# Delta rule: key and query products on halves of the TensorE rows

## The chip, the cores and the metric

The kernel runs on one NeuronCore of one Trainium2 chip. A core has five engines with instruction streams of their own: TensorE (PE in the profile, with its weight loads as PEld), VectorE (DVE), ScalarE (ACT), GpSimd (POOL) and SyncE (SP), which here only issues transfers. They meet through semaphores; sixteen DMA engines move data between the core's memory and HBM. The metric is device time in microseconds (us) of one execution; lower is better.

## The reference

A perceiver block on 128 sequences of 32 tokens, 512 channels: cross attention, a gated delta rule with an MLP behind it, and a feed-forward layer with quantised weights. The change concerns the delta rule only. It has 32 heads of 16 channels, and for each head:

```
q = l2norm(silu(silu(conv(h @ Wq.T))));  k = l2norm(silu(silu(conv(h @ Wk.T))))
v = silu(silu(conv(h @ Wv.T)));          beta = sigmoid(h @ Wbeta.T)
for t in range(32):                      # within each sequence
    err = S @ k[t] - v[t]
    S   = S - beta[t] * outer(err, k[t])
    o[t] = S @ q[t]
```

The kernel does not run this loop over a state. Within a sequence it forms the products k[s]·k[t] and k[s]·q[t] of all token pairs (a 32x32 block per head), solves the triangular system that the k·k block gives for 32 rows u, and gets the outputs as the masked k·q block times u.

## The kernel before, in words

The 4096 tokens stand as 8 groups of 512 (`NG`, `SG`), each of four tiles of 128 tokens; a tile holds four sequences of 32. The 512 channels are four chunks (`ec`) of 128, that is of 8 heads. Three stages follow each other, with some mixing at the borders: cross attention (to about 700 us), `delta_products` (about 704 to 1224 us), `delta_out_mlp` (to about 2415 us), and then the feed-forward layer `HadamardFfn`.

`delta_products` runs eight rounds, one a group (`a_round`). A round has 12 steps: four key and four query chunks, alternating, and then four value chunks. In each step `channels` does four matmuls of 128x128 by 512 tokens into a PSUM tile `pp` (L520), ScalarE copies the result with the convolution's last tap into `acc` (L525), VectorE adds the other three taps (L527), and ScalarE applies SiLU twice (L534, L535). Keys and queries of a chunk land in one tile `kq` [128 channels, 2, 512 tokens].

**Products.** TensorE sums over all 128 rows, but a product is wanted per head, over 16 rows. So the operand that moves is masked: for head h of a chunk, the tile `kqm` holds the keys and queries in that head's 16 rows and zeros in the other 112. `kqm` is [128, 8 heads, 2, 256 tokens], three such tiles exist; VectorE clears them once (L655) and afterwards `hold` writes only the 16 rows of each head, with eight transfers on SyncE's queue (L550). A piece is one chunk and 256 tokens; there are 8 pieces a group. `multiply` handles 128 tokens at a time through `products`: for each of the four sequences, the keys of 32 tokens are the stationary operand (128 rows, 32 columns), and the masked operand of the same 32 tokens, 8 heads by 2 by 32 = 512 columns, moves through (L455). The four matmuls write four strips of 32 partitions of one PSUM bank `pg`; they stand on four column strips of the array. ScalarE copies the bank to `kk` (L457), GpSimd sends the k·k half to memory (`ld`, L458), masks the k·q half (L461) and sends that (`pd`, L462). `psg` has two banks, `kk` six buffers.

The order is written out by hand and then refined by the scheduler of the framework, engine by engine. `tiles` says how many products follow the channel matmuls of each step (1, 2, 1, 1, 2, ...: 16 a round); the first round starts at step 4. In each round from the second on, `mixed` sets a share of the substitution (`Substitution.solve`, VectorE alone, L432 to L442) beside the steps; it reads `ld` of an earlier group.

**The last group.** Its keys and queries go to memory (`kd`) and `late_products` in `delta_out_mlp` does the 16 products of 128 tokens among the MLP's matmuls: three ahead of the first block, then two a block of 256 tokens. There one masked tile `km` [128, 8, 2, 128] and one `k` tile serve all; each product's eight masked transfers (L856) and its `k` (L858) wait until the product before has read its own.

Of the kernel before, what the change touches and what calls it, by code (L numbers as in the profile page):

```python
# [10 lines left out]
FP = mybir.dt.float32  # L11
# [7 lines left out]
P = 128  # L19
D = 512  # L20
DC = D // P
NB = 128
T = 32
# [4 lines left out]
HD = 16  # L28
TAPS = 4
SG = 512  # L30
# [355 lines left out]
GT = SG // P  # L386
GB = SG // T
H4 = 4
NC8 = H // H4
HH = 8  # L390
TB = 256
NTL = TB // P
# [54 lines left out]
        )  # L447


def products(nc, pg, pool, ld, pd, k, m, cm):  # L450


    for j in range(4):
        js = slice(j * T, (j + 1) * T)
        nc.tensor.matmul(pg[js], k[:, js], m[:, :, :, js], start=True, stop=True)  # L455
    kk = pool.tile([P, 2, HH, T], FP, name="kk")
    nc.scalar.copy(kk, pg.rearrange("p h n t -> p n h t"))  # L457
    nc.gpsimd.dma_start(  # L458
        ld.rearrange("c r f -> r c f"), kk[:, 0].rearrange("p (c h) t -> p c (h t)", c=2)
    )  # L460
    nc.gpsimd.tensor_mul(kk[:, 1], kk[:, 1], cm.unsqueeze(1).to_broadcast([P, HH, T]))  # L461
    nc.gpsimd.dma_start(pd, kk[:, 1].rearrange("p h t -> p (h t)"))  # L462


def delta_products(
# [8 lines left out]
    tc, nc = g.tc, g.nc  # L474
    KT = 256
# [6 lines left out]
    with stack:  # L482
# [33 lines left out]
        def channels(hT, n, ec):  # L516

            pp = psp.tile([P, GB, T], FP, name="pp")
            for dc in range(DC):
                nc.tensor.matmul(  # L520
                    pp.rearrange("p b t -> p (b t)"), w[n][:, dc, ec * P : (ec + 1) * P],
                    hT[:, dc, :], start=dc == 0, stop=dc == DC - 1,
                )
# [13 lines left out]


        pieces, held = [], []
        per = KT // P  # L540
        count = {"masked": 0, "done": 0}

        def hold():

            while len(held) < min(len(pieces), count["done"] // per + len(kqm)):
                gi, ec, half, kq = pieces[len(held)]
                m = kqm[len(held) % len(kqm)]
                for h in range(HH):
                    rows = slice(h * HD, (h + 1) * HD)
                    nc.sync.dma_start(m[rows, h], kq[rows, :, half * KT : (half + 1) * KT])  # L550
                held.append(m)

        def multiply():
            k = count["done"] // per
            gi, ec, half, kq = pieces[k]
            i = half * per + count["done"] % per
            t0 = count["done"] % per * P
            products(
                nc, psg.tile([P, HH, 2, T], FP, name="pg"), wk3,
                ld[gi, 2 * ec : 2 * ec + 2, i * P : (i + 1) * P], pd[gi, i, ec],  # L560
                kq[:, 0, i * P : (i + 1) * P], held[k][:, :, :, t0 : t0 + P], cm,
            )
            count["done"] += 1
            hold()
# [67 lines left out]


        todo = [(n, ec) for ec in range(DC) for n in "kq"] + [("v", ec) for ec in range(DC)]
        tiles = (1, 2, 1, 1, 2, 1, 1, 2, 1, 1, 2, 1)
        loads = (3, 4, 5, 9)

        def a_round(gi, old, hT, made):
            new = Group(gi)
            made.append(new)  # L640
            xt, kq = [], {}
            if gi + 1 < NG:
                hT_next = wk1.tile([P, DC, SG], FP, name="hT")
                made.append(hT_next)
            for j, (n, ec) in enumerate(todo):
                if n == "v":
                    dst = new.v[ec] = wk2.tile([P, SG], FP, name="v2", bufs=4)
                else:
                    if n == "k":
                        kq[ec] = wp3.tile([P, 2, SG], FP, name="kq")  # L650
                    dst = kq[ec][:, "kq".index(n)]
                acc, last = channels(hT, n, ec)
                with tc.issue_after(last):
                    for _ in range(min(HH, len(blank))):
# [39 lines left out]
        assert count["done"] == per * len(pieces)  # L694


def delta_out_mlp(
# [7 lines left out]
    tc, nc = g.tc, g.nc  # L705
# [6 lines left out]
    with stack:  # L712

        um = [bp.tile([P, H // 2, 2, 2 * HD], FP, name=f"um{i}") for i in range(2)]
        pe = [bp.tile([P, 2, 4, HH, T], FP, name=f"pe{i}") for i in range(2)]
        km = lp.tile([P, HH, 2, P], FP, name="km")
        for t in (*um, *pe, km):
            nc.gpsimd.memset(t, 0.0)
        cm = lp.tile([P, T], FP, name="cm")
# [13 lines left out]
        def back(b):  # L733

            gi, i0 = b * TB // SG, b * NTL % GT
            mv, rs = (t[:, b * NTL : (b + 1) * NTL] for t in stats)
            oT = wk.tile([P, NTL, DC, P], FP, name="oT", bufs=1)
            pm = psn.tile([P, NTL], FP, name="pm")
            xs = []
            for i in range(NTL):  # L740
# [6 lines left out]
                m = take("um", um)  # L747
# [4 lines left out]
                for c in range(DC):  # L752
                    if c % 2 == 0:
                        q2 = take("pe", pe)
                        for j in range(4):
                            js = slice(j * T, (j + 1) * T)
# [4 lines left out]
                    q = q2[:, c % 2]  # L761
                    for e in range(2):
                        for a in range(4):
# [3 lines left out]
                                start=e == 0, stop=e == 1,  # L767
# [4 lines left out]
                r = rp.tile([P, DC, P], FP, name="r")  # L772
# [33 lines left out]
            r = st.tile([P, NTL], FP, name="r")  # L806
# [42 lines left out]
        def late_products():  # L849

            gi = NG - 1

            def masked(ec, i):
                for h in range(HH):
                    rows = slice(h * HD, (h + 1) * HD)
# [7 lines left out]
            for n, (ec, i) in enumerate(todo):  # L863
# [492 lines left out]
```

## Time and profile before

| | us |
|---|---|
| median of three runs | 2990.05 |
| lowest, highest | 2984.76, 2990.45 |
| the profiled execution | 2991.72 |
| its span, first to last instruction | 2989.9 |
| TensorE busy in the span | 2879.6 |
| VectorE busy | 2008.9 |
| ScalarE busy | 1057.1 |
| GpSimd busy | 659.4 |

The profile is of one execution. A busy time is a union of intervals, and several matmuls may stand in the array at once. A group of instructions is shown with its line, engine, operation, the tile that it writes and reads, shapes, count, busy time, mean duration of one in ns, and the idle time ahead of it with what ended it. A float32 matmul of the program is two records[...], so 448 product matmuls of the rounds are 896 records. In the chain that ended last, each piece is given from the moment it became the last one running.

### The profile page before, as it was taken

How to read it: one execution, taken by the hardware profiler on the slowest of the kernel's cores; microseconds unless marked ns; L12 is line 12 of the kernel's file. 1: busy time of each engine (PE TensorE's matmuls, PEld its weight loads, DVE VectorE, ACT ScalarE, POOL GpSimd, SP SyncE). 2: the span in 40 equal slices, each digit the busy share in tenths (PEclk: the TensorE clock that was granted, in tenths of full speed). 3: DMA queues.
4: the chain of work that ended last, by engine and by line, in shares of the span. 5: the costliest groups of instructions: out<-in, count | busy, mean ns of one | idle time of the engine just before them, and what ended most of it. 6: DMA issues, size and time to landing. Idle time of an engine off the chain costs nothing.

```text
span 2989.9 us, 40853 instructions
## 1 busy us (share of the span) xinstructions
PE 2879.6 (96%) x14934; PEld 1649.2 (55%) x14934; DVE 2008.9 (67%) x3318; ACT 1057.1 (35%) x1777; POOL 659.4 (22%) x962
## 2 busy tenths in 40 slices
PE   8999999999999999699999999999999999999997
PEld 3434343443333333266666667777777756666664
DVE  2353544326599799358787878787822279999996
ACT  1111111114666666521122112111112137676674
POOL 1121212212676677221111111101010000000000
PEclk9999999999999999799999999999999999999999
DMA  9788997874545554741414131313141024434433
GB/s 326 259 310 272 342 311 253 290 256 119 167 119 149 163 148 120 219 142 55 128 55 135 55 119 53 119 55 101 43 140 50 20 71 80 89 85 86 90 70 67
DMA packets 342168, 428.47 MB, mean 143 GB/s; under 512 B 150224, under 2 KB 252752, under 8 KB 338512
## 3 DMA queue, kind: packets, MB, share of 16 engines
q1 hardware_dynamic: 305888, 325.93, 36.2%
q0 software_dynamic: 36080, 99.92, 10.9%
q8 instruction: 119, 1.95, 0.3%
q14 instruction: 81, 0.66, 0.1%
HBM read 288.36 MB, written 93.85 MB: 128 GB/s over the span
## 4 chain that ended last, share of the span: by engine, by line
PE 59%; DVE 5%; DMA 2%; issue 1%; ACT 1%; SPq 0%; POOL 0%; DVEq 0%; ACTq 0%; POOLq 0%
PE ps L909 17%; PE pm L823 9%; PE pm L834 9%; PE pm L826 9%; PE pp L520 5%; PE ps L797 4%; PE pg L455 2%; PE ps L764 2%; DVE W L442 1%; DVE pr L436 1%; DMA xs<-x 1%; PE ps L97 1%; DMA wd<-in_WdownT_dram 1%; DVE m L909 0%; PE pm L455 0%
## 5 line engine op out<-in xcount | busy, mean ns | idle before, releaser
L823 PE MATMUL pm<-hT,wg 128*128 128x256 f32 x1408 | 342.3, 386 | 0.2 <-ACT hT L812 0.2
L826 PE MATMUL pm<-hT,wu 128*128 128x256 f32 x1408 | 333.3, 379 | 0.0
L436 DVE TENSOR_TENSOR pr<-L,W 128x1984 f32<-128x1984 f32 (+30 forms) x248 | 312.6, 1261 | 24.6 <-DMA L<-ld 20.6
L442 DVE TENSOR_TENSOR W<-W,pr 128x1984 f32<-128x1984 f32 (+30 forms) x248 | 308.7, 1245 | 3.2
L834 PE MATMUL pm<-wd,mT 128*128 128x512 f32 x704 | 307.4, 592 | 0.0
L823 PEld LDWEIGHTS pm<-hT,wg 128*128 128x128 f32 x1408 | 262.1, 191 | 57.0 <-issue 16.2
L826 PEld LDWEIGHTS pm<-hT,wu 128*128 128x128 f32 x1408 | 267.2, 190 | 36.2
L834 PEld LDWEIGHTS pm<-wd,mT 128*128 128x128 f32 x704 | 132.4, 190 | 160.2 <-issue 159.8
L909 PE MATMUL ps<-wq,qT 128*128 128x512 bf16 x960 | 217.1, 379 | 3.0 <-ACT t L909 3.0
L828 ACT ACTIVATE sg<-pm 128x256 f32<-128x256 f32 x176 | 67.3, 383 | 344.8 <-PE pm L823 330.0
L829 DVE TENSOR_TENSOR mT<-pm,sg 128x256 f32<-128x256 f32 x176 | 73.7, 419 | 160.4 <-PE pm L826 147.0
L909 DVE TENSOR_TENSOR mb<-m 128x1024 f32<-128x1024 f32 x128 | 153.1, 1217 | 0.1
L909 DVE TENSOR_TENSOR m<-mb 128x1024 f32<-128x1024 f32 x128 | 150.7, 1219 | 1.2
L909 PEld LDWEIGHTS <-qT 128*128 128x128 bf16 x960 | 93.9, 98 | 103.7 <-issue 3.9
L1137 POOL DMA_DIRECT2D xo<-x x31 | 26.4, 851 | 528.1 <-ACT xo L909 512.1
L461 POOL TENSOR_TENSOR kk<-kk,cm 128x256 f32<-128x256 f32 x128 | 132.2, 1033 | 2.1
L909 ACT ACTIVATE t<-ps,magic,qs 128x512 f32<-128x512 f32 x158 | 115.7, 781 | 37.7 <-DVE qs L909 37.7
L909 PEld LDWEIGHTS ps<-hd,mT 128*128 128x128 f32 x1024 | 120.7, 194 | 8.9 <-ACT mT L909 4.8
L458 POOL DMA_DIRECT2D ld<-kk x128 | 92.7, 724 | 148.2 <-ACT kk L457 140.8
L909 PE MATMUL ps<-hd,mT 128*128 128x128 f32 x1024 | 121.4, 278 | 4.1 <-ACT mT L909 4.1
L346 PE MATMUL ps<-hT,wq 128*128 128x512 f32 x256 | 116.4, 614 | 7.8 <-ACT hT L339 7.8
L909 PE MATMUL ps<-wq,q2T 128*128 128x512 bf16 x512 | 120.2, 389 | 3.8 <-DMA q2T<-q 3.8
(225 smaller groups left out, 4841.1 us busy)
## 6 DMA issues: line engine op xcount, KB each, us to landing
kall<-in_ctxT_dram SPq DMA_DIRECT2D x32, 2056.0 KB
cx<-in_ctx_dram SPq DMA_DIRECT2D x32, 2048.0 KB
x<-xo POOLq DMA_DIRECT2D x64, 256.0 KB, 3.4
ld<-kk POOLq DMA_DIRECT2D x128, 128.0 KB, 2.6
pd<-kk POOLq DMA_DIRECT2D x128, 128.0 KB, 2.3
L<-ld SPq DMA_DIRECT2D x8, 2048.0 KB
pe<-pd SPq DMA_DIRECT2D x256, 64.0 KB
kqm<-kq SPq DMA_DIRECT2D x448, 32.0 KB
```

The costliest lines, as they stand in the source:

```text
L346: nc.tensor.matmul(pp, wn[:, dc, ec * P : (ec + 1) * P], hT[:, dc, :], start=dc == 0, stop=dc == DC - 1,)
L436: nc.vector.tensor_mul(pr[:, 0:n], bc(L[:, s, :, s + 1 : T].rearrange("p h t -> p t h"), HD), w[:, s].unsqueeze(1).to_broadcast([P, n, H4, ...
L442: nc.vector.tensor_sub(w[:, s + 1 :], w[:, s + 1 :], pr[:, 0:n])
L458: nc.gpsimd.dma_start(ld.rearrange("c r f -> r c f"), kk[:, 0].rearrange("p (c h) t -> p c (h t)", c=2))
L461: nc.gpsimd.tensor_mul(kk[:, 1], kk[:, 1], cm.unsqueeze(1).to_broadcast([P, HH, T]))
L520: nc.tensor.matmul(pp.rearrange("p b t -> p (b t)"), w[n][:, dc, ec * P : (ec + 1) * P], hT[:, dc, :], start=dc == 0, stop=dc == DC - 1,)
L797: nc.tensor.matmul(pw, oT[:, i, dc, :], wo[:, dc, :], start=dc == 0, stop=dc == DC - 1)
L823: nc.tensor.matmul(pg, wg[:, dc, fs], hT[:, dc, :], start=dc == 0, stop=dc == DC - 1)
L826: nc.tensor.matmul(pu, wu[:, dc, fs], hT[:, dc, :], start=dc == 0, stop=dc == DC - 1)
L829: mark[:] = [nc.vector.tensor_mul(mT[:, fc, :], pu, sg).ins]
L834: nc.tensor.matmul(pd, mT[:, fc, i * P : (i + 1) * P], wd[:, fc, :], start=fc == 0, stop=fc == FC - 1,)
L909: ins = method(*args, **kw).ins
```

## The change

The rows of the array are used in halves. A half holds four of a chunk's eight heads, so a masked operand needs only four slots: head h goes to slot h % 4, in its own 16 rows, and the zeros of a slot are now in the other three heads of each half. `kqm` becomes [128, 4, 2, 256], `km` [128, 4, 2, 256]. A matmul takes 64 rows of the keys and 4 x 2 x 32 = 256 moving columns, and writes to a bank of its half (`pgs[r]`). A call of `products` covers 256 tokens, with 16 matmuls: four sequences, two halves, two tiles of tokens. Each of its two banks is copied, masked and sent as before; a bank now holds 4 heads of 256 tokens instead of 8 heads of 128, and its `pd` transfer writes pieces of 512 bytes instead of 1024. The steps' list becomes `due` (at most one piece a step, 8 a round), the last group has 8 late products, two small statistics tiles get two buffers instead of four.

```diff
-def products(nc, pg, pool, ld, pd, k, m, cm):
-    for j in range(4):
-        js = slice(j * T, (j + 1) * T)
-        nc.tensor.matmul(pg[js], k[:, js], m[:, :, :, js], start=True, stop=True)
-    kk = pool.tile([P, 2, HH, T], FP, name="kk")
-    nc.scalar.copy(kk, pg.rearrange("p h n t -> p n h t"))
-    nc.gpsimd.dma_start(
-        ld.rearrange("c r f -> r c f"), kk[:, 0].rearrange("p (c h) t -> p c (h t)", c=2)
-    )
-    nc.gpsimd.tensor_mul(kk[:, 1], kk[:, 1], cm.unsqueeze(1).to_broadcast([P, HH, T]))
-    nc.gpsimd.dma_start(pd, kk[:, 1].rearrange("p h t -> p (h t)"))
+def masked_operand(nc, m, kq):
+    for h in range(HH):
+        rows = slice(h * HD, (h + 1) * HD)
+        nc.sync.dma_start(m[rows, h % H4], kq[rows])
+
+def products(nc, banks, pool, ld, pd, k, m, cm):
+    pgs = [banks() for _ in range(2)]
+    for i in range(2):
+        for r, pg in enumerate(pgs):
+            rows = slice(r * P // 2, (r + 1) * P // 2)
+            for j in range(4):
+                js = slice(j * T, (j + 1) * T)
+                ts = slice(i * P + j * T, i * P + (j + 1) * T)
+                nc.tensor.matmul(
+                    pg[js, :, i].rearrange("p n h t -> p h n t"), k[rows, ts], m[rows, :, :, ts],
+                    start=True, stop=True,
+                )
+    for r, pg in enumerate(pgs):
+        kk = pool.tile([P, 2, 2, H4, T], FP, name="kk")
+        nc.scalar.copy(kk, pg)
+        nc.gpsimd.dma_start(
+            ld[r].rearrange("(i p) f -> p i f", p=P), kk[:, 0].rearrange("p i h t -> p i (h t)")
+        )
+        q = kk[:, 1].rearrange("p i h t -> p (i h) t")
+        nc.gpsimd.tensor_mul(q, q, cm.unsqueeze(1).to_broadcast([P, 2 * H4, T]))
+        nc.gpsimd.dma_start(
+            pd[:, :, r * H4 * T : (r + 1) * H4 * T].rearrange("i p f -> p i f"),
+            kk[:, 1].rearrange("p i h t -> p i (h t)"),
+        )
@@ delta_products @@
-        kqm = [wp3.tile([P, HH, 2, KT], FP, name=f"kqm{i}", bufs=1) for i in range(3)]
-        blank = [t[:, h] for t in kqm for h in range(HH)]
+        kqm = [wp3.tile([P, H4, 2, KT], FP, name=f"kqm{i}", bufs=1) for i in range(3)]
+        blank = [t[:, h] for t in kqm for h in range(H4)]
...
         def multiply():
-            k = count["done"] // per
-            gi, ec, half, kq = pieces[k]
-            i = half * per + count["done"] % per
-            t0 = count["done"] % per * P
+            gi, ec, half, kq = pieces[count["done"]]
+            ts = slice(half * KT, (half + 1) * KT)
             products(
-                nc, psg.tile([P, HH, 2, T], FP, name="pg"), wk3,
-                ld[gi, 2 * ec : 2 * ec + 2, i * P : (i + 1) * P], pd[gi, i, ec],
-                kq[:, 0, i * P : (i + 1) * P], held[k][:, :, :, t0 : t0 + P], cm,
+                nc, lambda: psg.tile([P, 2, 2, H4, T], FP, name="pg"), wk3,
+                ld[gi, 2 * ec : 2 * ec + 2, ts], pd[gi, 2 * half : 2 * half + 2, ec],
+                kq[:, 0, ts], held[count["done"]], cm,
             )
...
-        tiles = (1, 2, 1, 1, 2, 1, 1, 2, 1, 1, 2, 1)
+        due = (0, 1, 1, 0, 1, 1, 0, 1, 1, 0, 1, 1)
...
-                for _ in range(tiles[j]):
-                    if count["done"] < per * len(held) and (old or j >= 4):
-                        multiply()
+                if due[j] and count["done"] < len(held) and (old or j >= 4):
+                    multiply()
@@ delta_out_mlp @@
-        km = lp.tile([P, HH, 2, P], FP, name="km")
+        km = lp.tile([P, H4, 2, TB], FP, name="km")
...
-            ro = st.tile([P, NTL], FP, name="ro")
+            ro = st.tile([P, NTL], FP, name="ro", bufs=2)
...
-            ms = st.tile([P, NTL], FP, name="ms")
+            ms = st.tile([P, NTL], FP, name="ms", bufs=2)
...
-            def masked(ec, i):
-                for h in range(HH):
-                    rows = slice(h * HD, (h + 1) * HD)
-                    nc.sync.dma_start(km[rows, h], kd[rows, ec, :, i * P : (i + 1) * P])
-                k = lp.tile([P, P], FP, name="k")
-                nc.sync.dma_start(k, kd[:, ec, 0, i * P : (i + 1) * P])
+            def masked(ec, b):
+                ts = slice(b * TB, (b + 1) * TB)
+                masked_operand(nc, km, kd[:, ec, :, ts])
+                k = lp.tile([P, TB], FP, name="k")
+                nc.sync.dma_start(k, kd[:, ec, 0, ts])
                 return k
-            todo = [(ec, i) for ec in range(DC) for i in range(GT)]
+            todo = [(ec, b) for ec in range(DC) for b in range(SG // TB)]
...
-                yield 1
+                yield 2
                 products(
-                    nc, psm.tile([P, HH, 2, T], FP, name="pm"), lp,
-                    ld[gi, 2 * ec : 2 * ec + 2, i * P : (i + 1) * P], pd[gi, i, ec], k, km, cm,
+                    nc, lambda: psm.tile([P, 2, 2, H4, T], FP, name="pm"), lp,
+                    ld[gi, 2 * ec : 2 * ec + 2, b * TB : (b + 1) * TB],
+                    pd[gi, NTL * b : NTL * (b + 1), ec], k, km, cm,
                 )
```

More of the change, by code (lines that the diff above doesn't have):

```diff
@@ L539, in delta_products @@
         pieces, held = [], []
-        per = KT // P
         count = {"masked": 0, "done": 0}
         def hold():
-            while len(held) < min(len(pieces), count["done"] // per + len(kqm)):
+            while len(held) < min(len(pieces), count["done"] + len(kqm)):
                 gi, ec, half, kq = pieces[len(held)]
                 m = kqm[len(held) % len(kqm)]
-                for h in range(HH):
-                    rows = slice(h * HD, (h + 1) * HD)
-                    nc.sync.dma_start(m[rows, h], kq[rows, :, half * KT : (half + 1) * KT])
+                masked_operand(nc, m, kq[:, :, half * KT : (half + 1) * KT])
                 held.append(m)
         def multiply():
-            k = count["done"] // per
-            gi, ec, half, kq = pieces[k]
-            i = half * per + count["done"] % per
-            t0 = count["done"] % per * P
+            gi, ec, half, kq = pieces[count["done"]]
+            ts = slice(half * KT, (half + 1) * KT)
             products(
-                nc, psg.tile([P, HH, 2, T], FP, name="pg"), wk3,
-                ld[gi, 2 * ec : 2 * ec + 2, i * P : (i + 1) * P], pd[gi, i, ec],
-                kq[:, 0, i * P : (i + 1) * P], held[k][:, :, :, t0 : t0 + P], cm,
+                nc, lambda: psg.tile([P, 2, 2, H4, T], FP, name="pg"), wk3,
+                ld[gi, 2 * ec : 2 * ec + 2, ts], pd[gi, 2 * half : 2 * half + 2, ec],
+                kq[:, 0, ts], held[count["done"]], cm,
             )
@@ L653, in a_round @@
                 with tc.issue_after(last):
-                    for _ in range(min(HH, len(blank))):
+                    for _ in range(min(H4, len(blank))):
                         nc.vector.memset(blank.pop(0), 0.0)
-                for _ in range(tiles[j]):
-                    if count["done"] < per * len(held) and (old or j >= 4):
-                        multiply()
+                if due[j] and count["done"] < len(held) and (old or j >= 4):
+                    multiply()
                 activated(acc, dst)
@@ L693, in delta_products @@
             old, hT = made[0], made[-1]
-        assert count["done"] == per * len(pieces)
+        assert count["done"] == len(pieces)
 def delta_out_mlp(
@@ L851, in late_products @@
             gi = NG - 1
-            def masked(ec, i):
-                for h in range(HH):
-                    rows = slice(h * HD, (h + 1) * HD)
-                    nc.sync.dma_start(km[rows, h], kd[rows, ec, :, i * P : (i + 1) * P])
-                k = lp.tile([P, P], FP, name="k")
-                nc.sync.dma_start(k, kd[:, ec, 0, i * P : (i + 1) * P])
+            def masked(ec, b):
[3 more added lines that the diff above has]
+                nc.sync.dma_start(k, kd[:, ec, 0, ts])
                 return k
-            todo = [(ec, i) for ec in range(DC) for i in range(GT)]
+            todo = [(ec, b) for ec in range(DC) for b in range(SG // TB)]
             k = masked(*todo[0])
-            for n, (ec, i) in enumerate(todo):
-                yield 1
+            for n, (ec, b) in enumerate(todo):
+                yield 2
                 products(
-                    nc, psm.tile([P, HH, 2, T], FP, name="pm"), lp,
-                    ld[gi, 2 * ec : 2 * ec + 2, i * P : (i + 1) * P], pd[gi, i, ec], k, km, cm,
+                    nc, lambda: psm.tile([P, 2, 2, H4, T], FP, name="pm"), lp,
+                    ld[gi, 2 * ec : 2 * ec + 2, b * TB : (b + 1) * TB],
+                    pd[gi, NTL * b : NTL * (b + 1), ec], k, km, cm,
                 )
```

## The prediction

> **What bounds the kernel now.** I read the page's first part, then the groups by form, then the rounds one by one, then the chain inside a round, and last who waits for whom.
>
> ```profile
> PE 2879.6 (96%) x14934; PEld 1649.2 (55%) x14934; DVE 2008.9 (67%) x3318; ACT 1057.1 (35%) x1777; POOL 659.4 (22%) x962
> ...
> L455 PE MATMUL pg<-kqm,kq 128*32 128x512 f32 x896 | 119.2, 601 | 2.4 <-DMA kqm<-kq 1.8 <-ACT kk L457 0.6
> ...
> L455 PE MATMUL pm<-km,k 128*32 128x512 f32 x128 | 19.8, 656 | 5.9 <-DMA km<-kd 2.6 <-DMA k<-kd 1.9 <-issue 1.4
> ```
>
> TensorE bounds the kernel as a whole; the products hold it for 119.2 + 19.8 = 139 us. The mean of 601 ns is a latency. Inside a burst the trace shows four records starting 7 ns apart, one a column strip, and the next four 0.429 us later; so one "slot" of four strips costs 0.429 us, and a product of 128 tokens (8 records) two of them.
>
> The eight rounds, each cut where its first channel matmul starts (columns: stretch, its length, busy time of each engine):
>
> ```profile
> core 0: us, PE busy (x) PEld busy (x) DVE busy (x) ACT busy (x) POOL busy (x), PEclk, DMA share, GB/s
> 704.50:766.60 62.10, 60.25 (x235) 22.30 (x232) 41.10 (x68) 40.11 (x60) 18.73 (x28) 1.00 0.37 103
> 766.60:832.70 66.10, 66.10 (x282) 24.78 (x278) 40.21 (x56) 44.81 (x67) 41.75 (x65) 1.00 0.57 173
> 832.70:904.70 72.00, 69.81 (x311) 25.48 (x310) 68.11 (x82) 44.67 (x72) 61.74 (x75) 1.00 0.47 133
> 904.70:971.30 66.60, 64.86 (x266) 24.12 (x266) 66.13 (x83) 39.73 (x60) 42.92 (x56) 1.00 0.50 144
> 971.30:1037.40 66.10, 66.10 (x281) 24.80 (x277) 49.26 (x85) 43.13 (x67) 42.12 (x65) 1.00 0.49 139
> 1037.40:1104.40 67.00, 67.00 (x285) 24.78 (x284) 62.84 (x72) 40.44 (x65) 49.75 (x68) 1.00 0.57 173
> 1104.40:1171.50 67.10, 67.10 (x286) 24.80 (x285) 65.32 (x80) 40.65 (x65) 44.80 (x63) 1.00 0.45 123
> 1171.50:1227.00 55.50, 54.31 (x185) 21.73 (x185) 32.75 (x51) 35.18 (x51) 29.09 (x40) 1.00 0.46 149
> ```
>
> This is the table that decides. TensorE is full in every round. But in rounds 2 and 3 VectorE is busy 134.2 of 138.6 us, and in 5 and 6 128.2 of 134.1, because the substitution stands beside them: a second engine is just behind the first there, and not in rounds 0, 1, 4 and 7.
>
> From the chain that ended last, round 5:
>
> ```profile
> 1070.19 3.63 PE pp L520 x8
> 1073.82 1.00 PE pg L455 x8
> 1074.82 3.63 PE pp L520 x8
> 1078.45 1.85 PE pg L455 x16
> ```
>
> The chain runs through the products. One takes 1.00, two 1.85: a second costs 0.85, two slots, and the rest is the way in. From starts in the trace, a channel matmul followed by its like loses 0.002 us; going from 128 columns to 32 or back loses 0.096.
>
> **What the Trainium skill says.** "TensorEngine Tiling (Array Packing)", Tiling Modes: 64x32 gives eight tiles that load and multiply independently, and a change of mode drains the array. The drain agrees: 0.096 us. Row halves at work together stand nowhere in this trace. The same page, Restrictions and Gotchas: row tiles may not write one PSUM bank at a time; hence the two banks. "TensorE: Matmul & The Clock Gate", Part 3: 16 tiles of 32x32 gained 10.6 times, for row packing; but it says that matmuls go strictly in program order, and the trace differs: each program matmul is two passes in a row, yet all four strips' first passes start ahead of any second pass. That lets me hope that the halves pass each other too. "PSUM — Partial Sum Buffer", Specifications: a non-contiguous pattern slows matmuls significantly. The new output goes in runs of 32 values; no row shows such a one.
>
> **The change, part by part.**
>
> *Slots.* Per 256 tokens and chunk, before: two products, 4 slots of 0.429 = 1.72 us. After: in the built program's order nearly every piece stands in one run, low half, high half, low, high, each with four strips. If the halves overlap, that is 4 slots (two passes, two tiles of tokens) of 256 columns. No row has 256 columns here; the slot is 0.109 us at 128 columns (L764), 0.243 at 289 (L255), 0.429 at 512, so 0.109 + 128 x 0.00083 = 0.2155 us (estimate from these). Eight starts at 7 ns need 0.06 us and fit. A piece: 0.86, so 0.86 less. The bounds: 0.86 gained with full overlap, nothing with none (8 slots). I take the full one. In round 0 the built order splits the first two pieces (all of the low half, channel matmuls, then the high half): 1.72 each.
>
> By round: round 0, 11 products of 0.858 become 4 x 0.86 + 2 x 1.72: 9.4 to 6.9, -2.5. Rounds 1 to 6: 13.7 to 6.9, -6.8 each. Round 7: 5 products become 2 pieces, 4.3 to 1.7, -2.6. In all -45.9. Changes of mode: I count 197 before and 189 after in this stage: 8 x 0.096 = -0.8 us.
>
> *What VectorE leaves of it.* Rounds 2 and 3: busy 134.2, and VectorE waited only 3.4 us there. The built order has 0.7 us more substitution in round 3; with 1 us of waits left, 135.9 against 138.6: -2.7 in place of -13.6. Rounds 5 and 6: 128.2, of which the new order moves about 3.4 us ahead into round 4 (by counts and lengths of L436 and L442); with 2 us of waits 126.8 against 134.1: -7.3 in place of -13.6. Its TensorE floor is 120.5. Round 4 has room (49.3 + 3.7 under 59.3), so -6.8; round 1 too. TensorE can't run ahead across a round's end: its transposes of the next tokens in steps 8 to 11 wait for VectorE's L511. Stage: -2.5 - 6.8 - 2.7 - 6.8 - 7.3 - 2.6 - 0.8 = -29.5 us.
>
> *Late products.* 16 x 2 x 0.429 = 13.7 us become 8 x 0.86 = 6.9: -6.8, since TensorE is 100% busy at 1300 to 1365. Early in this stage it waited 1.7 us for `km` (at 1280) and 2.0 for `k` (at 1289) between products; two larger pieces need one reload instead of three there: -2. Together -8.8. Their mask transfers fall from 144 to 72 on SyncE's queue, of twice the size.
>
> *Costed at nothing.* Half of the 24 clearings of 0.485 us go: VectorE is busy 41 of 62 us in round 0. ScalarE's copies stay at 128 of 0.58 us. The `pd` transfer gets 512-byte pieces as `ld` has, so its issue should go from 0.58 to 0.72 us on GpSimd: 16 x 0.14 = 2.3 us a round, covered by slack outside round 2 (61.7 busy of 72); there it would reach 64 of about 69. `kqm` transfers keep count and size. The smaller statistics buffers: uses of them are one MLP block apart.
>
> *A wait added.* A piece needs both `psg` banks at once, so it waits for the second copy of the piece before; behind it on TensorE stands the next step's channel matmul, for which ScalarE and then VectorE wait. Five of a round's pieces have one step of 3.44 us between them and the one ahead. Two copies take 1.2 us, and fit, unless a SiLU that waits for VectorE stands between (it does for about a third in ScalarE's built order). In the late products one `kk` buffer serves both banks, so the second copy waits some 4 us (copy, issue, mask, issue, landing 2.3), with the MLP's SiLUs behind it; the other four PSUM banks last two MLP columns, 7 us. Bounds: 0 to 15 us in all; I take 3.
>
> Sum: -29.5 - 8.8 + 3 = -35.3 on 2991.7, so 2956.4. The profiled execution stood 1.7 us above the median of the runs: 2955 us.
>
> **The rivals.**
>
> A, the above, VectorE taking over in four rounds: 2955, own range 2945 to 2966.
>
> B, TensorE's whole saving arrives, because VectorE slides work between rounds: -45.9 - 0.8 - 8.8 = -55.5: 2935. For it: VectorE has 26 idle us in round 1. Against: its order is fixed.
>
> C, the halves share a strip's queue, so that a half's second pass holds the other up: 5 slots a piece, 1.08 us. Rounds 0, 1, 4, 7 give 1.6 + 5.1 + 5.1 + 2.1, the other four the same 10.0, late products 5.1 + 2, changes 0.8, less 3: -28.8, 2961.
>
> D, the change doesn't do what it says: halves don't overlap. Eight slots of 0.2155 are the old 1.72 us. What is left is the reload and the mode changes, -2.8: 2987.
>
> E, slower: the pair of banks. If the wait for the second copy is the rule, because ScalarE's SiLUs behind a saturated VectorE stand ahead of it, each of 56 pieces stalls TensorE. From 35.3 / 56 = 0.63 us more a piece, nothing is gained; at 1 us more it is +20: 3010. For it: ScalarE waited 63.8 us for VectorE's convolution in rounds 1 to 6, 1.6 a time. Against: TensorE waited just 0.6 us for L457 in the group above.
>
> **How the numbers follow.** A 0.56, B 0.12, C 0.10, D 0.12, E 0.10. The likeliest gives 2955. To hold 8 in 10 the range takes A, C, most of B and the near half of D: 2932 to 2987. Within 0.2% means within 6 us, about what can be told here: D mostly. Faster: A, B, C and a part of D, 0.81; same 0.08; slower 0.11.
>
> **What would show it.** Right: eight product records starting within 0.06 us, the next eight 0.21 to 0.22 later; a burst of 32 records about 1.0 us in the chain; the product groups' busy time near 75 us instead of 139; rounds 1 and 4 near 59 us and rounds 2, 3, 5, 6 at 63 to 68 with VectorE over 95% busy and TensorE idle for L527. Wrong: starts in fours (D), five slots (C), or TensorE waiting for L475, the copy (E). A slot over 0.22 us would mean that runs of 32 in PSUM cost; at 0.43 all is lost. What would upset the sum most is VectorE's durations changing with GpSimd's, which share the rounds.

## The result, and the profile after

The changed kernel takes 2984.3 us (median of 20 runs) beside 2991.4 us of the kernel before, run in turn with it on the same chip: ratio 0.9973, 95% interval 0.9964 to 0.9983. That is 7 us of the 35 forecast. It lies inside the wide range of 2932 to 2987, near its slow end, but outside the 2945 to 2966 that the prediction gave for its own account, A. By the number alone it could be rival D (2987), whose mechanism the trace below excludes: that the wide range holds the result is luck. The profiled execution, one of the fastest of the 20, took 2975.98 us with a span of 2974.2, 15.7 us under the span before; between the medians there are only 7. 3.3 us of the 15.7 lie ahead of the changed stage (it starts at 701.3 instead of 704.6 us), in code that the change doesn't touch.

The page's first part after the change, and the groups of the products by form:

```profile
PE 2837.3 (95%) x15895; PEld 1661.6 (56%) x15958; DVE 2005.5 (67%) x3306; ACT 1040.4 (35%) x1769; POOL 676.0 (23%) x962
...
L469 PE MATMUL pg<-kqm,kq 64*32 64x256 f32 x1792 | 77.8, 387 | 15.7 <-ACT kk L475 14.7 <-DMA kqm<-kq 1.0
L469 PE MATMUL pm<-km,k 64*32 64x256 f32 x256 | 11.5, 414 | 2.6 <-DMA km<-kd 2.6
```

TensorE is busy for 42.3 us less (2879.6 to 2837.3), and the products hold it for 89 us instead of 139. So the work is gone. But the idle time in front of the products in the rounds, 2.4 us before, is 15.7 now, nearly all of it for ScalarE's copies (L475). In one burst eight product records start at 985.367 to 985.414, 7 ns apart, the next eight at 985.607, then 985.823 and 986.039: a first slot of 0.240 us and then 0.216. The halves do work side by side, and the slot is the one that the contiguous widths led to, so runs of 32 values in PSUM cost nothing that shows.

Not every piece runs so. Of the 56 pieces of the rounds 37 are four starts of eight records, nine are split by other matmuls, and ten begin with the low half alone. Most of these ten take six slots instead of four, like this one, whose high half waits for the copy (L475) of the second bank:

```profile
882.94 0.64 PE L469 MATMUL pg<-kqm,kq 64*32 64x256 f32 x8 [1.70 <-ACT kk L475]
883.95 1.07 PE L469 MATMUL pg<-kqm,kq 64*32 64x256 f32 x24 [0.37 <-ACT kk L475]
```

The rounds after the change, cut where each one's first channel matmul starts; the columns are the stretch, its length, each engine's busy time, the granted clock, DMA share and GB/s:

```profile
701.30:760.60 59.30, 58.22 (x341) 23.46 (x339) 38.01 (x60) 38.84 (x61) 23.25 (x33) 1.00 0.41 113
760.60:820.40 59.80, 59.09 (x403) 25.30 (x402) 35.29 (x49) 39.11 (x63) 42.29 (x61) 1.00 0.60 182
820.40:890.60 70.20, 62.75 (x422) 26.55 (x422) 70.00 (x82) 41.32 (x67) 54.27 (x72) 0.97 0.54 147
890.60:960.40 69.80, 63.61 (x414) 26.98 (x413) 68.02 (x89) 40.23 (x66) 49.07 (x65) 0.94 0.48 134
960.40:1024.90 64.50, 63.08 (x414) 26.64 (x413) 49.71 (x83) 39.80 (x65) 43.56 (x64) 0.96 0.56 162
1024.90:1094.60 69.70, 63.23 (x415) 26.52 (x414) 67.25 (x78) 41.03 (x66) 52.70 (x65) 0.98 0.56 159
1094.60:1162.40 67.80, 64.56 (x412) 27.06 (x411) 64.02 (x77) 39.62 (x65) 47.77 (x64) 0.97 0.43 114
```

Rounds 0 and 1 came down as forecast, 62.1 to 59.3 and 66.1 to 59.8. Rounds 2 and 3 together went from 138.6 to 140.0, rounds 5 and 6 from 134.1 to 137.5, round 4 only from 66.1 to 64.5. In rounds 2 and 3 VectorE is busy 138.0 of 140.0 us. The granted clock (the figure behind POOL's) has changed too: before it was 1.00 in every round, now it is below that from round 2 on.

Who waited for whom in rounds 2 to 6, before (832 to 1171 us) and after (820 to 1163); columns: total us, times, longest:

```profile
ACT acc L534 <- DVE acc L527: 54.1, 31, 3.5
PE ps L97 <- DVE hn L511: 1.9, 1, 1.9
```

```profile
ACT acc L556 <- DVE acc L549: 95.9, 47, 4.9
PE pg L469 <- ACT kk L475: 13.9, 12, 3.1
PE pn L595 <- ACT sq L593: 5.6, 5, 2.0
PE ps L97 <- DVE hn L533: 4.3, 2, 2.9
```

ScalarE waits nearly twice as long for VectorE's convolution, in front of its SiLUs; what stands behind these on ScalarE, the products' copies and the squares, is late, and TensorE waits for both. The sum of ScalarE's waits is no measure of the loss by itself (it is 114.8 us in the run below that keeps most of the gain; the longest is 4.9 us here and 3.2 there). The end of round 3 in TensorE's own order of time (start, length, group, and in brackets the idle time before it):

```profile
952.75 1.55 PE L469 MATMUL pg<-kqm,kq 64*32 64x256 f32 x32 [3.09 <-ACT kk L475]
954.24 0.46 PE L610 MATMUL ps<-ident,f 64*128 64x64 f32 x4
957.57 1.08 PE L97 MATMUL ps<-ident,hn 128*128 128x128 f32 x4 [2.87 <-DVE hn L533]
958.88 1.55 PE L469 MATMUL pg<-kqm,kq 64*32 64x256 f32 x10 [0.23 <-ACT kk L475]
960.36 6.13 PE L542 MATMUL pp<-hT,wk 128*128 128x512 f32 x8
```

Two stalls of 3 us, and behind them the same work takes longer: the channel matmul needs 6.13 us where one of the same eight records needs about 3.6. The records of the granted clock show half speed for 10.2 us from 955.1 on. Four such stretches stand in the rounds (6.8, 10.2, 6.8 and 3.4 us, from 886.8, 955.1, 1091.6 and 1163.3), each at stalls of a round's end: 1.70 and 1.44 us ahead of the first; 3.09 ahead of the second and 2.87 mostly inside it; 1.94, of which the first half lies ahead of the third; 1.37 and 1.86 ahead of the fourth. Before the change there was none in the rounds.

To add this up for the stage (first to last channel matmul, 519.4 us before, 512.4 after) I took the starts of all matmul records and split the time between two starts into what the columns need at full clock, changes of mode, half clock, and the rest, stalls. Work went from 479.4 to 439.9 us, changes of mode from 21.1 to 20.3, half clock from 0 to 10.0, and stalls, which hold the way into each burst too, from 19.2 to 42.4. So 40 us of work and mode changes went, and 33 us of waiting and slow clock came.

### The profile page after: what moved, and what is told of

Same layout as the page of the kernel before. It is cut to its first block, busy times and chain, and to the rows that moved or that the text cites. A ratio compares the mean times of both kernels' runs of the same rounds, so it can differ in the third digit from the quotient of the medians.

```text
span 2974.2 us, 42770 instructions
## 1 busy us (share of the span) xinstructions
PE 2837.3 (95%) x15895; PEld 1661.6 (56%) x15958; DVE 2005.5 (67%) x3306; ACT 1040.4 (35%) x1769; POOL 676.0 (23%) x962
## 4 chain that ended last, share of the span: by engine, by line
PE 59%; DVE 10%; DMA 3%; issue 2%; ACT 1%; POOL 1%; SPq 1%; DVEq 0%; ACTq 0%; POOLq 0%
PE ps L924 17%; PE pm L838 9%; PE pm L849 9%; PE pm L841 9%; PE pp L542 6%; PE ps L812 4%; DVE W L442 2%; DVE pr L436 2%; DVE acc L549 2%; PE ps L779 2%; PE pg L469 1%; DMA xs<-x 1%; DMA wd<-in_WdownT_dram 1%; PE pn L595 1%; SPq L455 0%
## 5 line engine op out<-in xcount | busy, mean ns | idle before, releaser
L843 ACT ACTIVATE sg<-pm 128x256 f32<-128x256 f32 x176 | 67.1, 382 | 326.2 <-PE pm L838 314.7
L542 PE MATMUL pp<-hT,wk 128*128 128x512 f32 x256 | 124.8, 632 | 0.7 <-ACT hT L536 0.7
L480 POOL TENSOR_TENSOR kk<-kk,cm 128x256 f32<-128x256 f32 x128 | 121.9, 953 | 2.6
```

Source lines behind the costliest of these rows:

```text
L480: nc.gpsimd.tensor_mul(q, q, cm.unsqueeze(1).to_broadcast([P, 2 * H4, T]))
L542: nc.tensor.matmul(pp.rearrange("p b t -> p (b t)"), w[n][:, dc, ec * P : (ec + 1) * P], hT[:, dc, :], start=dc == 0, stop=dc == DC - 1,)
```

## The experiments

My theory was (1): VectorE, loaded with the substitution in rounds 2 to 6, takes over at once, and this alone eats the gain. The rival was (2): the change is held by its own couplings, that is by ScalarE's copies of the pair of banks, by GpSimd's queue of masks and transfers, and by the half clock behind each stall, even where VectorE has time.

**Part of the substitution left out.** In `solve`, before and after:

```diff
-            if n:
+            if n and gi > 1:
```

Old products:

> The kernel before with most of the substitution left out for groups 0 and 1, the two that are solved beside the rounds: the multiply by beta stays, the updates by L do not, so VectorE loses some 120 us in rounds 1 to 6 (the output is then not the reference's). Every theory: TensorE was full there anyway, so rounds 1 to 6 stay at 66 to 67 us each, only the 4 to 5 us that rounds 2 and 3 were over go; 2980 to 2986 us.

New products:

> The changed kernel with the same work left out. Theory 1 (VectorE, with the substitution beside the rounds, is what kept TensorE's saving from arriving): rounds 1 to 6 fall to 59 to 60 us each, TensorE no longer waits for the copies to kk or for hn, its clock stays at full speed in the rounds, and the kernel is 50 to 56 us under before_light, about 2930. Theory 2 (the pair of banks, and ScalarE's copies, hold TensorE on their own account): TensorE still waits 10 us or more for the copies in rounds 2 to 6, rounds of 63 us and over, and the gain on before_light is 30 us or less.

Measured 2987.7 us (ratio to the kernel before 0.9988, 0.9975 to 1.0) and 2978.1 (0.9953, 0.9937 to 0.997), so the new products were worth 9.6 us. The edit also removed the `yield`s that hold the updates' place in the order, and so group 2's substitution moved up into rounds 4 and 5 (VectorE 62.0 and 67.8 us busy there). Rounds 1, 2, 3 and 6, free of substitution, came to 61.5, 62.6, 66.8 and 62.5 instead of 59.3. Round 3 shows that (1) is not all: VectorE is busy for 41 of 66.8 us there, and TensorE still stalls, behind a `vt` (L637) that waited 4.3 us for its transfer.

**Two that don't answer their question.** The first issues each product matmul of rounds 2, 3, 5 and 6 twice, to keep TensorE's clock up:

> The changed kernel, but in rounds 2, 3, 5 and 6 every product matmul is issued twice (the same values to the same places), which gives TensorE back the work that it had before there, 6.9 us a round. Theory 1 with the clock: those rounds stay at VectorE's pace, 67 to 70 us, TensorE has no long gaps at their ends, the four stretches of half clock (27 us in the changed kernel's rounds) go, and round 4 falls from 64.5 to 59 to 60; the kernel gets 5 to 12 us faster than the changed one although it does more. If the half clock costs nothing because TensorE has time to spare: same as the changed kernel within 3 us. If TensorE's work still sets those rounds: slower by up to 27 us.

3026.2 us (1.0125, 1.0106 to 1.0144). The scheduler moved more substitution into rounds 2 and 3, which took 85.4 and 86.3 us with VectorE busy for 84.9 and 77.6, and a clock of 0.95 and 0.91. Round 2 grew by the 15 us that VectorE's load grew by; on the clock the run says nothing. The second lowers the share of substitution beside the rounds, and allows 40 cost units of it ahead of the first MLP block:

```diff
-SHARE = 0.27 * SOLVE
+SHARE = 0.20 * SOLVE
...
```

> The changed kernel with less substitution beside the rounds: the share per round 0.20 of a solve in place of 0.27, and 40 of its cost units put ahead of the first MLP block, where VectorE is busy only 40 of 83 us. Theory 1: rounds 2, 3, 5 and 6 lose some 6 us of VectorE work each and come to 61 to 64 us, round 4 to 60; stage of the rounds 20 us shorter, the later stage the same or up to 5 us longer; 2962 to 2970. Theory 2: rounds unchanged, 2980 to 2988.

2990.4 us (1.0, 0.9987 to 1.0012), VectorE's load in rounds 2, 3, 5 and 6 as before (68.0, 68.9, 63.1, 67.1). The same 49 pairs of updates stand in rounds 1 to 6 as without the edit; the share written in the code doesn't bind the scheduler.

**No substitution beside the rounds.** The updates of the first two groups are left out again, so the kernel computes something else, but now their place in the order is kept:

```diff
-            if n:
+            if n and gi < 2:
+                yield 0.3 + 0.07 * n
+            elif n:
```

Old products, new products, and new products with four `vt` buffers (`bufs=4` on its tile):

> Leaves out the updates by L of the first two groups but keeps their place in the order, so that no substitution stands beside the rounds; products as before. Both theories: VectorE about 40 us busy in each of rounds 2 to 6, TensorE full; rounds 2 to 6 at its floor of about 66.1 us each (72.0 and 67 before in those that VectorE filled), the products' stage some 8 to 10 us shorter than before, the whole about 2983. No half-clock stretch in the rounds.

> The same with the changed products. Theory 1 (the substitution on VectorE takes all of the lost gain): rounds 1 to 6 at 59.3 us, six times 6.8 us under the run with the old products, stalls of TensorE under 3 us a round, no half-clock stretch; the whole about 50 to 55 us under that run, some 2930. Theory 2 (ScalarE's copies of the pair of banks, GpSimd's queue and the half clock after each stall hold it even with VectorE free): at least 3 of these rounds stay at 62 us or more, with waits of TensorE for the copies L477 of 2 to 3 us each, and the gain stays under 35 us.

> As the run before, with four buffers for vt instead of two. Theory 2a (vt waits for its transfer behind the products' mask and transfers on GpSimd, which holds VectorE, then ScalarE's copies, then TensorE): 5 us or more under the run with two buffers, VectorE's waits for the vd transfer gone. Theory 1, or if the copies alone are the cause: within 2 us of it.

2987.8 us (0.9988, 0.9977 to 1.0), 2960.4 (0.9908, 0.9888 to 0.9928) and 2950.4 (0.9872, 0.9852 to 0.9892). With the substitution gone the change is worth 27.4 us, with more `vt` buffers too 37.4, instead of 7. (The old products without substitution were not run with four buffers; TensorE is busy in all of their rounds 1 to 6, so there is next to nothing for buffers to save there.) The products' stage: 516.6, 487.0, 476.6 us. Rounds 3 to 5 of the three:

```profile
898.20:965.40 67.20, 67.20 (x285) 24.86 (x284) 37.82 (x70) 44.57 (x67) 41.94 (x65) 1.00 0.58 176
965.40:1032.60 67.20, 67.20 (x285) 24.85 (x284) 35.60 (x52) 44.62 (x67) 41.57 (x65) 1.00 0.59 175
1032.60:1099.80 67.20, 67.20 (x285) 24.85 (x284) 35.89 (x52) 44.64 (x67) 41.66 (x65) 1.00 0.47 128
```

```profile
889.60:954.00 64.40, 60.67 (x413) 25.74 (x412) 39.85 (x70) 40.03 (x65) 43.86 (x65) 1.00 0.61 178
954.00:1020.40 66.40, 62.34 (x413) 26.24 (x412) 35.80 (x52) 40.26 (x65) 43.70 (x65) 0.97 0.60 178
1020.40:1083.10 62.70, 61.88 (x413) 26.23 (x412) 35.62 (x52) 40.18 (x65) 43.71 (x65) 0.97 0.51 137
```

```profile
891.20:952.70 61.50, 60.11 (x413) 25.61 (x412) 37.89 (x70) 40.03 (x65) 43.78 (x65) 1.00 0.63 188
952.70:1013.70 61.00, 60.18 (x413) 25.63 (x412) 35.62 (x52) 40.18 (x65) 43.73 (x65) 1.00 0.65 194
1013.70:1074.70 61.00, 60.18 (x413) 25.63 (x412) 35.62 (x52) 40.17 (x65) 43.73 (x65) 1.00 0.52 142
```

The middle one has no engine near full but TensorE, and yet loses 1.7 to 5.4 us a round against the last. Two of the long pieces of its chain in round 4 (start, length, what):

```profile
954.12 3.63 PE pp L544 x8
961.18 8.07 DMA vd<-vt
```

The `vd` transfers stand on GpSimd's queue behind the masks and transfers of the products. VectorE's `vt` waits for a buffer that such a transfer still holds, the convolution stands behind `vt`, ScalarE's SiLU behind the convolution, the copies behind the SiLU, and TensorE behind the copies. Waits from 763 to 1150 us with two buffers, and with four:

```profile
ACT acc L558 <- DVE acc L551: 121.4, 67, 8.0
PE pg L471 <- ACT kk L477: 11.9, 8, 3.2
DVE vt L639 <- DMA vd<-vt: 7.6, 4, 5.1
```

```profile
ACT acc L558 <- DVE acc L551: 114.8, 70, 3.2
PE pg L471 <- ACT kk L477: 5.3, 6, 1.4
```

With four buffers VectorE's waits for this transfer are gone. No piece begins with the low half alone any more: 48 of the 56 are four starts of eight, with the same two banks. So both theories hold a part: of the 46.7 us that I reckoned as TensorE's saving in the stage, 40.0 can be had (516.6 to 476.6); without more buffers it is 29.6, with the substitution in place 7.0.

**More `vt` buffers alone.**

> Old products, four buffers for vt instead of two, nothing else. TensorE is full in every round of the kernel before, so both theories expect no more than the 1 to 3 us of the stalls at the stage's ends: 2986 to 2990.

> Changed products, four buffers for vt instead of two. If the vt loop costs what it cost without the substitution, 10 us: 2972 to 2976, with rounds 3 to 6 shorter. If VectorE's own work fills rounds 2, 3, 5 and 6 (96 to 100% busy), its waits there are too few to give more than 3 us back: 2979 to 2983.

2990.1 us (0.9998, 0.9987 to 1.0008) and 2982.1 (0.9972, 0.9961 to 0.9983). Beside the full VectorE the buffers give nothing that can be told: the loop through `vt` showed a cost only where VectorE has room.

**The substitution spread.** Each update is tied to the convolution of the step it is set beside, so the scheduler can't move it ahead; less of it stands beside the rounds, and 30 of its cost units ahead of the first MLP block:

```diff
-SHARE = 0.27 * SOLVE
+SHARE = 0.19 * SOLVE
...
                 acc, last = channels(hT, n, ec)
+                g.mark = [last]
...
-            mixed((len(todo), a_round(gi, old, hT, made)), *beside(gi))
+            mixed(
+                (len(todo), a_round(gi, old, hT, made)),
+                *((cost, after_taps(g, steps)) for cost, steps in beside(gi)),
+            )
```

(`after_taps` draws each step of the substitution inside `issue_after(g.mark[0])`, as `behind` does in the MLP stage.)

> The whole computation, with the changed products; the substitution is tied to the channels' convolution so that it can't be moved ahead, 0.19 of a group beside each round instead of 0.27, and 30 units of it at the start of the MLP stage, where VectorE is idle. Theory 1: VectorE is busy 54 to 58 us a round, rounds 2 to 6 come to 59 to 62 us each, against 64 to 70 now, and with the later stage no longer than now the whole is 2950 to 2962. Theory 2: stalls for the copies stay, rounds 2 to 6 at 63 to 67 us, the whole 2970 to 2985.

2982.4 us (0.9979, 0.9969 to 0.9989). The rounds did come down, to 64.8, 64.8, 62.9, 65.1 and 62.8 us, with VectorE at 48.8 to 56.4, and the stage to 493.2. But the 30 units ahead of the MLP stood in front of that stage's first work on VectorE: its first matmul came 68.4 us behind the last channel matmul instead of 57.5, and the later stage grew from 1185.8 to 1205.4. A miss of placement. Then 0.22, 8 units, 50 units beside the first block, and four `vt` buffers, with the old and with the new products:

> Old products with the pinned substitution (0.22 of a group beside a round, 8 units ahead of the first MLP block, 50 instead of 45 beside it) and four buffers for vt. TensorE at its floor of 66.1 to 67.2 us in rounds 1 to 6: the whole 2978 to 2986.

> The same order and buffers with the changed products. If the change's gain was lost to VectorE and to the vt loop alone: VectorE 57 to 59 us busy in rounds 2 to 6, these at 60 to 62 us, 30 us or more under the run with the old products: 2945 to 2955. If the half clock and the copies of the pair of banks hold it on their own: rounds at 63 to 66, less than 20 us under that run.

2997.3 us (1.002, 1.0011 to 1.0029) and 2969.6 (0.9943, 0.9922 to 0.9964). In the same order and with the same buffers the new products are worth 27.7 us instead of 7. The order itself costs the old products some 6 us, so beside the kernel before it is 21.6; this version beats both kernels. The stage is 517.2 and 495.1 us. It isn't the 30 us and more that I wrote, and the rounds are not at 60 to 62 but where I had put them for half clock and copies that hold TensorE on their own:

```profile
820.30:884.80 64.50, 60.98 (x423) 25.90 (x423) 54.98 (x65) 40.15 (x65) 49.86 (x69) 1.00 0.58 154
884.80:948.20 63.40, 61.82 (x413) 26.42 (x412) 54.64 (x67) 40.49 (x65) 46.88 (x64) 0.97 0.53 144
948.20:1012.50 64.30, 61.80 (x416) 26.11 (x415) 57.73 (x75) 39.92 (x65) 50.86 (x66) 0.99 0.52 141
1012.50:1077.70 65.20, 63.06 (x412) 26.80 (x411) 58.42 (x87) 40.49 (x65) 45.06 (x65) 0.96 0.49 129
1077.70:1144.10 66.40, 61.48 (x413) 26.01 (x412) 57.12 (x71) 40.83 (x65) 51.21 (x65) 1.00 0.62 181
```

VectorE is busy for 55 to 58 us a round, TensorE needs about 60, and the round takes 63 to 66: my reading, which no run tests, is that with two engines this close an update of 1.5 to 2 us on VectorE that comes at the wrong moment is a stall of TensorE.

**ScalarE's order.** What is left in that version are six waits of TensorE for the copies, 11.2 us in all. So the copies were put right behind the channels' copy of their step, with the SiLUs tied behind them and moved a step later:

```diff
+                if pending:
+                    with tc.issue_after(copied) if copied else ExitStack():
+                        pending.pop()()
```

(`pending` holds the step's `activated` and what hangs on it; `acc` gets four buffers.) With nothing else changed, and with the spread substitution:

> Changed products; only ScalarE's order is altered: the copies of the two banks stand right behind the channels' copy of their step, and each step's two SiLUs follow a step later, tied behind them. If TensorE's waits for the copies (30 us between 820 and 1163, with the half clock behind them) are a loss of their own: rounds 3, 5 and 6 lose 2 to 5 us each and no half clock is left: 2968 to 2976. If VectorE's work fills these rounds whatever ScalarE does (138.5 and 135.9 us in each pair): within 4 us of the changed kernel, 2980 to 2986, with the waits of TensorE only under another name.

> The pinned substitution (0.22 a round, 8 units, 50 units), four vt buffers and ScalarE's order together, with the changed products. If SiLUs that wait for VectorE in front of the copies are what is left: rounds 2 to 6 from 64.8 to 60 to 62 us each, no waits for L475's counterpart over 1 us, half clock under 2 us: 2948 to 2958. If the half clock and the stalls have another source: 2964 to 2972.

2987.9 us (1.0002, 0.9992 to 1.0012) and 2975.7 (0.995, 0.9931 to 0.9969). TensorE's waits for the copies shrink to one of 1.4 us in the first and to none in the second, but two waits of 6.9 us in all for the copy of `hT` (L537) come up in the first, and nothing is gained. In its stage stalls and half clock are 34.3 and 8.8 us (42.4 and 10.0 without), but the work and the changes of mode grow by 7.5: the copies' new place splits more pieces, and only 35 of the 56 are four starts of eight in one burst. Rounds 5 and 6 come down from 137.5 to 133.1, while rounds 2 and 3 take 139.8, VectorE busy for 136.3 of them, as theory (1) has it: there the wait for the copies is where the loss shows, not where it arises. For the other rounds the run doesn't settle it, since it changed the bursts along with the order; and no run gave the pairs more banks.

**The late products alone,** in the kernel before:

> The kernel before with only the late products changed (halves side by side, masked operand half as long, two statistics buffers). The prediction's step: -8.8 us, 2982. The profile of the changed kernel gave -4.8 in that stage, and its half-clock stretches came in the MLP's odd blocks; if these come from the late products themselves, -4 to 0: 2987 to 2991.

2991.3 us beside 2988.0 (1.0007, 0.9999 to 1.0015): no gain. The MLP blocks by the starts of their last matmuls: the first ends 8.5 us earlier in the profile (126.7 instead of 135.2 us behind the last channel matmul, though other runs of the old form have 132.5 to 135.5). Blocks 1, 3 and 5, beside which the next attention output is made, take 75.0, 75.5 and 80.2 us instead of 74.3, 73.1 and 72.9. In block 3 (1495 to 1575 us) TensorE's waits, before and here:

```profile
PE pm L783 <- DVE sq L782: 1.1, 1, 1.1
```

```profile
PE pm L820 <- DVE sq L819: 2.7, 1, 2.7
```

With less of its own to do, TensorE reaches the sum of squares earlier, VectorE (62 of 75 us busy in that stretch) doesn't have it sooner, and half clock follows (0.98 granted there, 1.00 before).

Block 5, which loses most, shows a second cause. ScalarE's second copy of a pair waits until the `pd` transfer has left the one `kk` buffer, and the MLP's next matmuls (L863), ScalarE's square (L817) and, through that, VectorE's sum of squares (L818, L819) wait behind it:

```profile
1659.94 0.58 ACT L490 COPY kk<-pm 128x512 f32<-128x512 f32 x1 [8.08 <-DMA pd<-kk]
1660.58 2.00 PE L863 MATMUL pm<-hT,wu 128*128 128x256 f32 x8 [2.23 <-ACT kk L490]
1661.09 0.84 DVE L818 TENSOR_TENSOR sq<-sq 128x256 f32<-128x256 f32 x1 [3.71 <-ACT sq L817]
1666.52 0.59 PE L820 MATMUL pm<-inv_d,sq 128*128 128x1 f32 x2 [3.51 <-DVE sq L819]
```

From 1225 to 1670 us these copies wait nine times for a `pd` transfer, 36.9 us in all here and 34.6 in the changed kernel; in the kernel before they wait for the product itself instead:

```profile
ACT kk L457 <- PE pm L455: 50.7, 11, 6.4
```

```profile
ACT kk L490 <- DMA pd<-kk: 36.9, 9, 8.1
```

How much of the lost gain a second `kk` buffer would bring back, no run shows.

## Why the prediction was wrong

The step that failed is what the prediction calls "What VectorE leaves of it": it let rounds 2, 3, 5 and 6 gain 10 us and took round 4 as free (-6.8). The four rounds lost 4.8 us together, and round 4 gained 1.6. The mechanism, VectorE taking over, was there, but its cost was mis-sized: a nearly full VectorE gave none of the gain back. And the delays that pass from it through ScalarE to TensorE were put at 3 us and the slow clock at nothing; together they came to 33 us of the stage.

- **The slots: right in the main.** 0.2155 us a slot was forecast from three other widths and measured at 0.216. Theories C and D are out: in the burst above eight records start together, and the piece is four slots. Full overlap held for 37 of 56 pieces; in ten the low half ran ahead, which the prediction did not have. The trace differs here from "TensorE: Matmul & The Clock Gate" of the Trainium skill, Part 3, which has matmuls go strictly in program order; and "PSUM — Partial Sum Buffer", Specifications, says that any non-contiguous pattern slows matmuls significantly, which runs of 32 values did not (0.216 us). The product groups hold TensorE for 89 us, not 75; in the run with four `vt` buffers and no substitution, where no piece began with one half alone, it is 80.5.
- **Rounds 0 and 1: right,** -2.8 and -6.3 for -2.5 and -6.8. Round 7 gave -1.2 for -2.6, behind a half-clock stretch at its start.
- **"What VectorE leaves of it": failed.** For rounds 2 and 3 I took 135.9 and got 140.0. The substitution there is 71.1 us (70.2 before), near what I read. But VectorE's other work there grew by 2.9 us: round 1 is cut where TensorE starts the next, TensorE got there 6 us sooner, and what VectorE still owed to round 1 (3.2 us less of it now stands in round 1) fell into round 2. For 5 and 6 I took 126.8 and got 137.5. I had 3.4 us of substitution move into round 4; the trace has +0.4 there and +3.6 in 5 and 6 (65.3 to 68.9), most of it from round 7. And I left 2 us of waits for 6.2. That the overdue work of round 1 fell into round 2 is read from the trace; no run tested it alone.
- **Round 4, taken as free: failed, -1.6 for -6.8.** VectorE has room there (49.7 us), but the round begins in half clock (2.4 us by the split) behind the stalls of round 3, and its chain goes through a `vd` transfer for 2.7 us (at 986.15).
- **"A wait added": named, and sized at 3 us.** The stalls grew by 23 us and the half clock by 10 in the stage. Rival E had the place right: TensorE waits for L475, the sign that the prediction set for E, behind SiLUs that wait for VectorE. Its price of 1 us a piece was much too high: 13.9 us in twelve waits from 820 to 1163 us. The pair of banks by itself is not the cause, since with the same pair TensorE waits only 5.3 us (763 to 1150 us) once VectorE and its `vt` buffers are free.
- **"Late products": -8.8 forecast.** The profile of the changed kernel has -4.8 in that stage; alone the step gave nothing. The wait of the second copy for the one `kk` buffer was named, at some 4 us each, and came nine times, 34.6 us of ScalarE's time; the prediction put all its added waits at 3 us.
- **The half clock: missing altogether.** "TensorE: Matmul & The Clock Gate", Part 1, puts the fall to half clock behind about 3.4 us of idle time; here it came at stalls of 1.4 to 3.1 us, mostly two within a few us. I gave it no price; by the split it cost 10 us of the stage.

By these steps in the profiled stage: forecast -29.5, found -7.0. Rounds 2 and 3 are 4.1 us of the difference, 5 and 6 10.7, round 4 5.2, the others 2.5. They are of one execution of each kernel.

## What to carry to other kernels

Where one engine was full and a second 96 to 97% busy in the same rounds, the first one's gain there was nothing until the second's work was taken away. So look at rounds, not at sums, and expect what the second engine owes to an earlier round to fall into the next. A TensorE that became faster than its suppliers paid twice here, once in stalls (23 us more in the stage) and once in half clock (10 us). Run the change also beside a neighbour with room: that told here that the change, with two more buffers for `vt`, was good for 37 us and its surroundings took 30.

## What was not expected of the hardware

Half clock came in steps of 3.4 us of the record. Within one profile the stretches of it all start on one grid of 3.413 us, that is, a whole number of such steps apart: in the changed kernel the four of the rounds start 20, 40 and 21 steps apart and last one to three steps, and in the kernel before and the run with the late products alone it is the same. No single length of a stall decides: one of 2.3 us beside MLP block 1 was followed by half clock in the run with the late products alone, one of 2.3 us in the same stretch of the kernel before was not. The first lay in one step of its grid (1369.0 to 1372.5), the second was spread over two. The idle time in a step doesn't decide by itself either: in the changed kernel TensorE was busy for 1.42 of 3.41 us in the step from 948.2 and the next step had full clock, and for 2.11 in the step from 1088.2 and the next had half. That the stalls cause it is argued from this order in time; no run took the one away and kept the other.

And eight matmuls on eight tiles of 64 rows by 32 columns start 7 ns apart and go through in slots of 256 columns, 0.216 us each, though the program gives each half's matmuls, of two records each, one after the other. Where the second half's bank comes late, the first half runs two slots ahead.
